# A quarter of the FFN's inner layer on 32-column places of the TensorE array

## The chip, the cores and the metric

The kernel runs on one core of one Trainium2 chip. The metric is device time in microseconds, from one launch; the time before is the median of three runs.

## The reference

The input x has 10000 rows of 512 values. A graph layer comes first (message passing over 5000 edges, two linear layers with batch norm and SiLU), then a mixture-of-experts layer. The change touches only the second, which with tokens normalised per row and grouped by 16 is:

```python
cont_logits = einsum('bgtd,des->bgtes', grouped, controller) + tie
cont_perm = (cont_logits == max(cont_logits, axis=-3, keepdims=True))
intermediate = einsum('bgtd,desf->bgtesf', grouped, f1)
inner = relu(einsum('bgtesf,bgtes->bgesf', intermediate, cont_perm))
inter2 = einsum('bgesf,esfd->bgesd', inner, f2)
result = einsum('bgesd,bgtes->bgtd', inter2, cont_perm)
```

There are 16 x 4 = 64 expert sets (called experts here). In each group of 16 tokens each expert picks the token with the largest logit, multiplies it by its own 512 x 32 matrix (the inner layer), and by its own 32 x 512 matrix (the outer layer); the result goes back to the token that was picked.

## The kernel before

The graph layer fills about the first 1278 us. The FFN follows: its 10000 tokens are cut into 20 chunks of 512 (`CH`; the last has 272), each with `G` = 32 groups of 16 tokens. Matrices `f1_sb` and `f2_sb` stay in SBUF.

A loop of `step` calls works as a pipeline written out by hand: one call (a round) handles five chunks at different stages. Chunk `a` is normalised, transposed (`flip`) and gets its logits and choice; chunk `b` gathers the picked tokens and runs the inner layer; chunk `d` runs the outer layer; chunk `e` is turned and scattered back; later chunks load. Inside the FFN each engine's instructions keep their program order (`InOrder`; all such instructions have the line 525 of that helper in the profile, so they are told apart by their tiles).

The part around the change goes over `k`, the four 128-row slices of the 512 inputs:

```python
gat(1); inn(0); turns(2, 4)
gat(2); inn(1); turns(4, 6)
gat(3); turns(6, 8); silu(0); silu(1)
inn(2); silu(2); silu(3)
inn(3); put(b, Chunk.relu); put(e, Chunk.scatter, 0)
```

(written here in fewer lines). `gather(k)` multiplies token tiles `xl` by the one-hot table `bd` on TensorE into PSUM (`pb`), and ScalarE copies the result to `gs`: for slice k, 128 inputs by 64 experts by 32 groups. `inner(k, gs)` multiplies this by `f1_sb` and adds up over k in the PSUM tile `pi`, two banks of 128 partitions by 16 blocks `m` by 2 by 32 groups. A block m holds four experts, and is computed in two matmuls, one for q = 0 (partitions 0 to 63) and one for q = 1 (partitions 64 to 127). Each has the weights of two experts (s = 0 and 1, 2 x 32 = 64 array columns) and as moving operand the tokens of both (2 x 32 = 64 columns). So each matmul yields four 32 x 32 squares, and two of them, the weights of one expert with tokens of the other, are not used: `relu` reads only rows 64q + 32s with column half s. The two matmuls lie on different columns of the array, and are free to run side by side.

`outer` then reads the result `ib` with matmuls of 32 rows by 32 columns; `scatter` uses 64 rows by 32 columns, `gather` 32 rows by 128 columns, `logits` 128 by 64, `flip` and `residual` are transposes of 128 by 128. The profile writes these shapes as 32*32, 64*32, 32*128, 128*64 and 128*128, and behind them the rows by the moving columns.

Of the kernel before, what the change touches and what calls it, by code (L numbers as in the profile page):

```python
# [18 lines left out]
NEX, SETS, F = 16, 4, 32  # L19
# [4 lines left out]
KH = H // P  # L24
# [26 lines left out]
def gnn_ffn_kernel(ctx: ExitStack, tc: tile.TileContext, a: dict, out: bass.AP):  # L51
# [126 lines left out]
    with tc.tile_pool(name="pe1", bufs=1) as pe1, tc.tile_pool(name="pe", bufs=2) as pe, \  # L178
# [31 lines left out]
        for r0 in range(0, AGG_ROWS, 8 * P):  # L210
            j = min(8, (AGG_ROWS - r0) // P)
# [39 lines left out]
        for g in range(groups):  # L251
            row = targets(g)
            for i in range(EG):
                t = g * EG + i
# [27 lines left out]
        for g in range(groups):  # L282
# [3 lines left out]
            for i in range(EG):  # L286
                t = g * EG + i
                nc.vector.tensor_scalar(same[i], row[:, :i + 1, :], dst_f[:, t:t + 1], None, op0=ALU.is_equal)
            rs, sh = ln
            for i in range(EG):  # L290
                t = g * EG + i
# [8 lines left out]
            for i in range(EG):  # L300
                t = g * EG + i
                pc = ps_e.tile([TE, H], F32, name="pc", bufs=3)
                for k in range(i, EG):
                    nc.tensor.matmul(pc, lhsT=same[k][:, i, :], rhs=xgs[g * EG + k], start=(k == i),
                                     stop=(k == EG - 1))
# [204 lines left out]
    f1_sb = wf.tile([P, KH, ES * F], F32, name="f1_sb")  # L510
# [16 lines left out]
    pe, dve, act, pool = (InOrder(e) for e in (nc.tensor, nc.vector, nc.scalar, nc.gpsimd))  # L527

    class Chunk:
# [148 lines left out]
        def inner(self, k, gs):  # L678


            if k == 0:
                self.pi = ps_i.tile([P, MF, 2, G], F32, name="pi")
            gs = gs.rearrange("p (t u q s b) g -> p t u q b s g", t=2, u=4, q=2, s=2)
            for m in range(MF):
                for q in range(2):
                    b, t = m // 2, m % 2
                    j = 4 * b + 2 * q + t
                    pe.matmul(self.pi[64 * q:64 * q + 64, m], lhsT=f1_sb[:, k, 2 * F * j:2 * F * (j + 1)],
                                     rhs=gs[:, t, b // 2, q, b % 2],
                                     start=(k == 0 and m % 8 == 0), stop=(k == KH - 1), skip_group_check=True)  # L690

        def relu(self):

# [268 lines left out]
```

## Time and profile before

| | us |
|---|---|
| median of three runs | 1968.99 (1967.05 to 1970.73) |
| the profiled execution | 1968.09 |
| its span, first to last instruction | 1966.4 |
| start of the first inner-layer matmul | 1278.8 |
| TensorE busy, share of the span | 1792.2, 91% |
| VectorE busy | 1207.8, 61% |
| ScalarE busy | 722.5, 37% |
| GpSimd busy | 621.5, 32% |
| inner-layer matmuls busy | 165.9, 5120 records of 225 ns mean |
| mean granted TensorE clock | 0.967 |

A record is one entry of the trace. TensorE's records overlap: the mean of one is from its start to its end, and neighbours on other columns or rows run beside it, so 5120 records of 225 ns come to 165.9 us of busy time. What a record costs in a stream is the distance between starts, not its length. In the page's lines PE is TensorE's matmuls, PEld its weight loads, DVE VectorE, ACT ScalarE, POOL GpSimd, SP the queue that issues DMAs; `<-` after an idle time names what ended it.

### The profile page before, as it was taken

What the parts mean: (1) busy time and instruction counts of PE and PEld (TensorE: products, weight loads), DVE (VectorE), ACT (ScalarE), POOL (GpSimd) and SP (SyncE); (2) the same over time, 40 slices, a digit from 0 to 9 for tenths busy, and PEclk for the clock granted to TensorE, in tenths of its full rate; (3) what the DMA queues carried; (4) which work ended last, traced back from release to release, by engine and by line L of the source; (5) the groups of instructions that cost most, each with busy time, mean ns of one, the idle gap of its engine ahead of it and who ended that gap; (6) DMA issues with size and microseconds to landing.
All of it is one profiled execution on the core that took longest, in us unless ns stands there. A gap on an engine that the chain in (4) does not pass through costs nothing. (4 is left out here: it accounts for less than half of the span.)

```text
span 1966.4 us, 43924 instructions
## 1 busy us (share of the span) xinstructions
PE 1792.2 (91%) x19354; PEld 1029.4 (52%) x19354; DVE 1207.8 (61%) x1894; ACT 722.5 (37%) x973; POOL 621.5 (32%) x626
## 2 busy tenths in 40 slices
PE   5959399999999997999999999589999999999985
PEld 2424144444444443444444444367777777777763
DVE  8547276777777767434334334327787777777766
ACT  0324233333333315222222220255555555555432
POOL 4275333333233314333333331122323232323311
PEclk9979599999999998999999999699999999999998
DMA  9997444443444312333333331742232323232101
GB/s 349 301 228 143 99 169 170 162 158 151 162 162 162 140 42 84 125 147 128 143 125 126 125 126 42 237 129 88 87 112 79 120 79 120 80 119 70 45 24 57
DMA packets 95219, 256.37 MB, mean 130 GB/s; under 512 B 7845, under 2 KB 8435, under 8 KB 94452
## 3 DMA queue, kind: packets, MB, share of 16 engines
q1 hardware_dynamic: 86068, 232.58, 32.5%
q0 software_dynamic: 8960, 20.98, 5.3%
q8 instruction: 152, 2.49, 0.5%
q14 instruction: 39, 0.32, 0.0%
HBM read 143.47 MB, written 110.07 MB: 129 GB/s over the span
## 5 line engine op out<-in xcount | busy, mean ns | idle before, releaser
L133 PE MATMUL x<-h_s,w_u 128*128 128x500 f32 x640 | 289.1, 584 | 0.3 <-POOL h_s L123 0.3
L525 ACT COPY gs<-pb 128x1024 f32<-128x1024 f32 (+2 forms) x168 | 161.5, 1027 | 123.6 <-PE pb L525 112.0
L133 PEld LDWEIGHTS x<-h_s,w_u 128*128 128x128 f32 x640 | 122.4, 191 | 148.2 <-issue 142.9
L525 DVE STREAM_TRANSPOSE it<-it 128x1024 f32<-128x1024 f32 x152 | 174.9, 1209 | 0.1
L525 PE MATMUL pi<-gs,f_sb 128*64 128x64 f32 x5120 | 165.9, 225 | 3.3 <-ACT gs L525 1.7
L525 POOL TENSOR_TENSOR pv<-perm,odd_t 64x512 f32<-64x512 f32 (+1 forms) x80 | 99.8, 1248 | 206.8 <-PE pb L525 178.2
L525 PEld LDWEIGHTS pi<-gs,f_sb 128*64 128x64 f32 x5120 | 157.3, 140 | 11.0 <-issue 2.2
L525 PE MATMUL pb<-bd,xl 32*128 32x128 f32 x2504 | 144.7, 285 | 15.1 <-ACT it L525 8.8
L143 DVE SCALAR_TENSOR_TENSOR t<-w,s 128x500 f32<-128x500 f32 x60 | 40.7, 678 | 188.5 <-PE w L133 184.8
L133 PE MATMUL z<-h_s,w 128*128 128x500 f32 x320 | 148.3, 586 | 3.9 <-POOL h_s L123 3.9
L525 PE MATMUL pb<-f_sb,ib 32*32 32x256 f32 x5120 | 134.7, 385 | 14.2 <-ACT it L525 8.6
L525 DVE COPY it<-pb 128x1024 f32<-128x1024 f32 x76 | 93.1, 1225 | 88.6 <-PE pb L525 88.5
L133 PE MATMUL z<-h_s,w_u 128*128 128x500 f32 x320 | 144.0, 583 | 0.3 <-POOL h_s L123 0.3
L525 PEld LDWEIGHTS pb<-bd,xl 32*128 32x128 f32 x2504 | 129.0, 188 | 27.7 <-ACT it L525 13.6
L123 POOL TENSOR_TENSOR h_s<-hc 128x500 f32<-128x500 f32 x60 | 77.0, 1316 | 149.1 <-PE z L133 149.1
L525 ACT COPY it<-pb 128x1024 f32<-128x1024 f32 x76 | 79.0, 1039 | 112.1 <-PE pb L525 112.1
L138 ACT COPY s<-z 128x500 f32<-128x500 f32 x60 | 34.5, 575 | 220.2 <-PE z L133 156.4
L525 POOL TENSOR_SCALAR ln_rs<-ln_mv 128x4 f32<-128x4 f32 (+2 forms) x22 | 4.9, 224 | 302.5 <-DVE ln_mv L525 302.4
L525 PEld LDWEIGHTS pb<-f_sb,ib 32*32 32x32 f32 x5120 | 70.2, 103 | 57.1 <-ACT it L525 14.6
L133 PEld LDWEIGHTS z<-h_s,w_u 128*128 128x128 f32 x320 | 60.8, 190 | 73.9 <-issue 72.7
L123 POOL TENSOR_TENSOR h_s<-hb 128x1000 f32<-128x1000 f32 x30 | 69.6, 2335 | 91.5 <-PE z L133 65.3
L433 DVE BATCH_NORM_STATS2 st<-h 128x6 f32<-128x500 f32 x144 | 93.7, 671 | 1.3
(180 smaller groups left out, 3084.9 us busy)
## 6 DMA issues: line engine op xcount, KB each, us to landing
h1s<-h SPq DMA_DIRECT2D x36, 1000.0 KB
agg<-zero SPq DMA_DIRECT2D x10, 2048.0 KB
xt<-in_x_dram SPq DMA_DIRECT2D x20, 1000.0 KB
hc<-h1s SPq DMA_DIRECT2D x20, 1000.0 KB
h2s<-h SPq DMA_DIRECT2D x20, 1000.0 KB
x<-in_x_dram SPq DMA_DIRECT2D x39, 512.0 KB
out_dram<-x SPq DMA_DIRECT2D x39, 512.0 KB
yt<-h2s SPq DMA_DIRECT2D x76, 256.0 KB
```

The lines of the kernel that those rows point to most:

```text
L123: eng.tensor_tensor(t[:, k0:k1], q(*x0, k0, k1), q(*x1, k0, k1), op)
L133: nc.tensor.matmul(bank, lhsT=us[n][:, k, m * P:(m + 1) * P], rhs=bs[n][k], start=start and k == 0, stop=k == kb - 1, skip_group_check=True)
L138: nc.scalar.copy(kept[n], banks[n])
L143: nc.vector.scalar_tensor_tensor(dst, banks[x0], sc, kept[x1], op0=op, op1=ALU.add)
L433: nc.vector.bn_stats(out=st1[:, 4 * r + m, 2 * i + t, :], in_=h1[:, r, t, :])
L525: return lambda *args, **kw: tc.keep_in_program_order(f(*args, **kw))
```

## The change

In `inner`, of each four blocks the second (m = 1, 5, 9, 13) is computed with one expert to a matmul: four matmuls, each with 32 array columns (one expert's weights) and 32 moving columns (the same expert's tokens), on the four 32-column places of the array. The squares that nobody reads are no longer computed in these blocks. The other twelve blocks stay at two matmuls of 64 columns. The order over m and q, the PSUM tile and its readers stay.

```diff
             for m in range(MF):
+                b, t = m // 2, m % 2
+                alone = m % 4 == 1
                 for q in range(2):
-                    b, t = m // 2, m % 2
-                    j = 4 * b + 2 * q + t
-                    pe.matmul(self.pi[64 * q:64 * q + 64, m], lhsT=f1_sb[:, k, 2 * F * j:2 * F * (j + 1)],
-                                     rhs=gs[:, t, b // 2, q, b % 2],
-                                     start=(k == 0 and m % 8 == 0), stop=(k == KH - 1), skip_group_check=True)
+                    es = 8 * b + 4 * q + 2 * t
+                    for s in (0, 1) if alone else (slice(0, 2),):
+                        e0, e1 = (es + s, es + s + 1) if alone else (es, es + 2)
+                        c0 = 64 * q + F * (e0 - es)
+                        pe.matmul(self.pi[c0:c0 + F * (e1 - e0), m, s], lhsT=f1_sb[:, k, F * e0:F * e1],
+                                  rhs=gs[:, t, b // 2, q, b % 2, s],
+                                  start=(k == 0 and m % 8 == 0), stop=(k == KH - 1), skip_group_check=True)
```

## The prediction

> **What bounds the kernel now.** I read the page's busy table first, then the busy time of two rounds of the FFN loop, then TensorE's waits in that loop, then the order of time on TensorE.
>
> The busy table and the group that the change edits (busy us, mean ns of one; then the engine's idle time before them):
>
> ```profile
> PE 1792.2 (91%) x19354; PEld 1029.4 (52%) x19354; DVE 1207.8 (61%) x1894; ACT 722.5 (37%) x973; POOL 621.5 (32%) x626
> ...
> L525 PE MATMUL pi<-gs,f_sb 128*64 128x64 f32 x5120 | 165.9, 225 | 3.3 <-ACT gs L525 1.7
> ```
>
> TensorE is busy 91% of the span. The inner layer has 5120 records for 20 chunks x 4 slices of D x 32 matmuls = 2560 matmuls, so each fp32 matmul is two records ("passes" below). They began only 3.3 us late in total. 128*64 says 128 rows and 64 columns of the array; 128x64 says 64 moving columns.
>
> Busy time by stretch, two rounds of the loop (a round handles one chunk per stage and takes about 32.8 us):
>
> ```profile
> core 0: us, PE busy (x) PEld busy (x) DVE busy (x) ACT busy (x) POOL busy (x), PEclk, DMA share, GB/s
> ...
> 1600.00:1633.00 33.00, 31.87 (x819) 24.38 (x818) 24.96 (x34) 18.53 (x23) 9.82 (x12) 1.00 0.32 99
> ...
> 1700.00:1733.00 33.00, 32.21 (x826) 24.77 (x824) 25.23 (x34) 18.64 (x23) 9.81 (x12) 1.00 0.31 100
> ```
>
> TensorE is busy 32.2 of 33.0 us at a granted clock of 1.00; VectorE, the next, 25.2. What TensorE waited for in the loop, 1300 to 1900 us (total us, times, longest):
>
> ```profile
> PE pb L525 <- ACT it L525: 13.1, 32, 1.1
> ...
> PE pb L525 <- ACT gs L525: 0.6, 1, 0.6
> ```
>
> The only wait of size is in the outer layer, for a PSUM buffer that ScalarE empties; around the inner layer there is next to none. So TensorE bounds the loop, and time added to the inner layer adds to the round.
>
> Now TensorE in order of time (start us, length us):
>
> ```profile
> 1602.36 2.09 PE L525 MATMUL pi<-gs,f_sb 128*64 128x64 f32 x64
> 1604.37 1.72 PE L525 MATMUL pb<-bd,xl 32*128 32x128 f32 x32
> ...
> 1609.69 3.95 PE L525 MATMUL pi<-gs,f_sb 128*64 128x64 f32 x128
> 1613.57 0.67 PE L525 MATMUL pb<-it,pv 64*32 64x256 f32 x16
> ```
>
> A run of 64 inner records takes 1604.37 - 1602.36 = 2.01 us until the next kind starts, one of 128 takes 3.88. The difference, 1.87 us for 64, makes 29.2 ns a record; two places of 64 columns work side by side, so a pair takes 58.4. What is left, 2.01 - 1.87 = 0.14 us, is paid once a run, whatever its length. It is the price of changing the shape of the array. Two other kinds give it as well:
>
> ```profile
> 1617.20 1.09 PE L525 MATMUL ps<-ident,xl 128*128 128x128 f32 x8
> 1618.22 1.90 PE L525 MATMUL pb<-f_sb,ib 32*32 32x256 f32 x64
> ...
> 1620.06 0.65 PE L525 MATMUL pi<-xlt,ctl 128*64 128x256 f32 x4
> 1620.64 0.66 PE L525 MATMUL ps<-ident,xl 128*128 128x128 f32 x4
> ...
> 1621.23 0.65 PE L525 MATMUL pi<-xlt,ctl 128*64 128x256 f32 x4
> ...
> 1623.82 1.08 PE L525 MATMUL pi<-xlt,ctl 128*64 128x256 f32 x8
> 1624.83 0.66 PE L525 MATMUL ps<-ident,yt 128*128 128x128 f32 x4
> ```
>
> Transposes (128*128): eight take 1.02 us, four 0.59, so 0.43 for four more and 0.16 a run. Logits (128*64, 256 moving columns): eight take 1.01, four 0.58, so 0.43 for four more and 0.15 a run. Both have 128 rows: a change of column size alone, from 64 to 128 or back, pays 0.15 us too, though no row size changed.
>
> **The change part by part.** In each of the 80 calls of `inner` (20 chunks x 4 slices), blocks m = 1, 5, 9 and 13 turn from two matmuls of 64 array columns and 64 moving columns into four of 32 and 32: 80 x 4 = 320 changed blocks. 640 matmuls go, 1280 come; TensorE gets 640 more matmuls, which is 1280 more records, each with a weight load. The order of instructions on VectorE, ScalarE, GpSimd and the DMA queue is the same before and after; no wait is added, and buffers, `relu` and all readers of `pi` stay. [...]So the whole sum is TensorE's.
>
> *Removed:* 4 records a block, 4 x 29.2 = 117 ns.
>
> *Added records:* 8 a block on four places. No row shows 128*32 with 32 moving columns (four transposes of the last chunk have 128*32, with 128 columns on one place). By the slope of the rows: a pair of 256-column records takes 0.43/2 = 215 ns, a pair of 64-column ones 58.4, so 0.816 ns a moving column, and 58.4 - 32 x 0.816 = 32.3 ns at 32. If four places work at once, two passes take 65 ns; this is the low end, since faster would mean streaming faster than any row. If only two places ever overlap, four sets take 129: the high end. Between them lies the nearest kind with 32-column places and short operands, the last scatter:
>
> ```profile
> 1955.18 1.18 PE L525 MATMUL pb<-f_sb,pv 64*32 64x64 f32 x64 [0.99 <-DVE f_sb L525]
> ```
>
> (1.18 - 0.31) / 63 = 13.8 ns a record (0.31 us is the mean of one in its group), 110 ns for eight, but with twice the moving columns and eight places. I take 80 ns: the low end, plus some 13 ns because four starts follow each other at about 6.5 ns, as the two of a pair do now.
>
> A rule bears on this. The Trainium skill, "TensorE: Matmul & The Clock Gate", section "Wait — 56ns, not 53.3ns?", says that start to start never drops below about 25 ns however small the matmul. The row above has 13.8 ns on separate places, so the floor does not hold from place to place; I go by the row. By the rule the eight records would take 200 ns, and my sum would rise by 0.12 x 308 = 37 us.
>
> *Added changes of shape:* every changed block lies between blocks of 64 columns (m = 0 and 15 are not changed). The run is broken twice, into 32 columns and back: 640 more changes. For the way back I take 0.14, the price of the inner layer's own runs. For the way in, no row has this pair of shapes; the three prices are 0.14 to 0.16, and they contain the first weight load, which is shorter for fewer columns (means of 103, 140 and 190 ns for 32, 64 and 128 columns). I take 0.13, with 0.12 and 0.16 as ends. Below that, to nothing, is the third rival.
>
> A second rule speaks for the change: the Trainium skill, "TensorEngine Tiling (Array Packing)", section "Theoretical Speedup", gives up to 4x for a dimension of 32 or less against up to 2x at 64. Blocks would fall to half, 117 to 59 ns, 320 x 58 = 19 us saved. The run prices above are what it leaves out: 270 ns a block stand against those 58.
>
> *Sum per block:* 0.13 + 0.14 + 0.080 - 0.117 = +0.233 us, or 3.7 us a round of 16 blocks.
>
> *What hides some.* In the last round the chunk has 272 tokens and TensorE waits for ScalarE's copies:
>
> ```profile
> 1914.07 2.09 PE L525 MATMUL pi<-gs,f_sb 128*64 128x64 f32 x64 [1.66 <-ACT gs L525]
> ```
>
> The 12 changed blocks of the first three slices there run inside such waits, the last four do not. 320 - 12 = 308 blocks x 0.233 = 72 us. In the other rounds I count nothing hidden: the next gather, and then the scatter, follow the inner layer with no wait. VectorE and ScalarE get later work and more slack. At most the idle 0.8 us of each round, 18 x 0.8 = 14 us, could be taken up, if waits for `it` shrank; I use it for the low end only. Next late is VectorE's `relu`, which waits for `pi`, and with it everything in the following round by the same 3.7 us.
>
> The sum is against the profiled execution: 1968.09 us (span 1966.4 and 1.7 around it), 0.9 below the median of 1968.99, which is inside the spread of the runs. The same difference on the median: 1969 + 72 = 2041 us.
>
> **The rivals.**
>
> 1. *Forecast:* each changed block pays two changes of shape. 2041 us. Chance 0.80.
> 2. *Records in line:* 25 ns each by the rule, or places that hold each other up: 0.13 + 0.14 + 0.20 - 0.117 = 0.353, x 308 = 109, so 2078 us. For it: rule, and 110 ns for eight in the scatter where streaming alone would allow less. Against it: 13.8 ns a record. Chance 0.05.
> 3. *One change of shape free:* 32-column places lie inside the 64-column ones, so only one of the two directions might pay: 0.14 + 0.080 - 0.117 = 0.103, x 308 = 32, so 2001 us. Against: transposes and logits pay both ways. Chance 0.06.
> 4. *No price between 64 and 32 columns* (the other side; also if both widths run in the same shape, so that the change is less than it says): 0.080 - 0.117, or 0.065 - 0.117, x 320 = -12 to -17, so 1952 to 1957 us. It decides at the price of a change of shape: with 80 ns of records a block breaks even at (117 - 80) / 2 = 18 ns a change. The cheapest of three kinds is 140. Chance 0.09.
>
> **How the numbers follow.** Low end of the forecast: 0.12 + 0.14 + 0.065 - 0.117 = 0.208 x 308 = 64, less the 14 us of idle time: +50, 2019 us. High end: 0.16 + 0.16 + 0.129 - 0.117 = 0.332 x 308 = 102, 2071 us; I stop at 2070. Rivals 2 to 4, together 0.20, lie outside. A difference below 0.2% (4 us) can't be told from none. Slower by more than that: cases 1 to 3 less a sliver, 0.90; within it 0.01; faster 0.09.
>
> **What would show it.** Right: the inner layer's records fall into two groups, 128*64 x3840 and 128*32 x2560; a round grows from 32.8 to about 36.5 us; from the last record of 64 columns to the first of 32 there are about 150 ns (58 within a run), and some 0.12 back; the other engines' busy times stay. Wrong: records of 32 columns starting 50 ns or less after those of 64 (rival 4), or in only one direction late (rival 3), or 25 ns apart from each other (rival 2); or a round that grows by much less than 16 x 0.233 us while TensorE's waits for `it` shrink, which would say that I took too little as hidden.

## The result, and the profile after

| | before | changed |
|---|---|---|
| median of six runs, us | 1966.2 (1964.8 to 1970.7) | 2060.3 (2051.5 to 2067.9) |
| profiled execution, us | 1968.09 | 2054.67 |
| its span, us | 1966.4 | 2053.0 |
| mean granted TensorE clock in it | 0.967 | 0.953 |

The changed kernel is slower: ratio 1.0474, 95% interval 1.044 to 1.0508, or 94 us between the medians and 86.6 between the two profiled spans. The forecast was +72, so the time lies inside the stated range and above its middle. The runs of the changed kernel also spread wider, 16 us against 6.

The busy table of the changed kernel's page, and its two inner-layer groups with shapes kept apart:

```profile
PE 1883.9 (92%) x20634; PEld 1076.6 (52%) x20634; DVE 1205.6 (59%) x1894; ACT 720.8 (35%) x973; POOL 623.0 (30%) x626
```

```profile
L525 PE MATMUL pi<-gs,f_sb 128*64 128x64 f32 x3840 | 203.8, 239 | 1.4 <-issue 1.4
...
L525 PE MATMUL pi<-gs,f_sb 128*32 128x32 f32 x2560 | 87.6, 210 | 0.0
```

TensorE has 20634 - 19354 = 1280 more records, split as announced, 3840 and 2560. VectorE, ScalarE and GpSimd are busy as long as before to within 2.2 us. All of the time is in TensorE's stream.

A round in the middle of the loop, by busy time (columns as before), and TensorE's waits between 1310 and 1890 us:

```profile
1606.60:1643.10 36.50, 35.71 (x888) 26.54 (x886) 25.02 (x34) 18.56 (x23) 9.85 (x12) 1.00 0.26 90
```

```profile
PE pb L525 <- ACT it L525: 11.6, 30, 0.6
PE ps L525 <- DVE x L525: 1.2, 2, 1.0
PE pi L525 <- ACT xlt L525: 0.9, 1, 0.9
```

The same waits of the kernel before:

```profile
PE pb L525 <- ACT it L525: 12.1, 31, 0.5
PE ps L525 <- issue: 1.4, 2, 0.8
PE pi L525 <- ACT xlt L525: 0.9, 1, 0.9
PE pb L525 <- ACT gs L525: 0.6, 1, 0.6
```

A round takes 36.5 us in place of 32.8. The waits for `it` total 11.6 us; before, they were 12.1. So no wait gave room for the added time. In order of time, the same round:

```profile
1606.88 3.00 PE L525 MATMUL pi<-gs,f_sb 128*64 128x64 f32 x80
1609.82 1.72 PE L525 MATMUL pb<-bd,xl 32*128 32x128 f32 x32
...
1616.05 5.79 PE L525 MATMUL pi<-gs,f_sb 128*64 128x64 f32 x160
1621.77 1.53 PE L525 MATMUL pb<-it,pv 64*32 64x256 f32 x48
```

(Both shapes are merged in these lines, under the name of the first.) A call until the next gather takes 1609.82 - 1606.88 = 2.94 us; it was 2.01. The difference, 0.93 us, over four blocks is 0.23 us a block. The weight loads of its first blocks, of which the first of each line starts 2 ns before its matmul (the last line stops after six):

```profile
1606.88 0.20 PEld L525 LDWEIGHTS pi<-gs,f_sb 128*64 128x64 f32 x4
...
1607.14 0.16 PEld L525 LDWEIGHTS pi<-gs,f_sb 128*32 128x32 f32 x8
...
1607.34 0.26 PEld L525 LDWEIGHTS pi<-gs,f_sb 128*64 128x64 f32 x6
```

Single starts in the trace show where the time goes, the same to 1 ns at every change in the loop at full clock. The first 32-column record starts 152 ns after the last 64-column one (52 from pair to pair inside a run). The four places start 7 ns apart, and their second pass 52 ns after the first. The first 64-column record starts 126 ns after the last 32-column one, and the next pair 100 ns after that pair (again 52 inside a run). Streaming takes some 53 ns for 64 columns and 27 for 32, estimated from the 215 ns that 256 columns take in the logits; so 99 ns are left at each change, in either direction, in which nothing starts. The late second passes, 48 ns for 64 columns and some 20 for 32, fit a first weight load that nothing covers; that was not tried by itself.

The rounds at the two ends behave otherwise. These are stretches of the kernel before, the first round and then everything from the start of the last inner layer:

```profile
1278.80:1309.70 30.90, 23.20 (x438) 19.18 (x436) 8.90 (x20) 14.24 (x19) 4.71 (x8) 1.00 0.58 176
1901.70:1966.40 64.70, 40.67 (x1326) 27.98 (x1324) 43.20 (x37) 17.18 (x26) 8.23 (x8) 0.90 0.12 44
```

and the same two of the changed kernel:

```profile
1279.80:1317.90 38.10, 34.03 (x500) 25.97 (x498) 8.84 (x20) 14.19 (x19) 4.73 (x8) 0.73 0.43 134
1972.20:2053.00 80.80, 59.97 (x1390) 37.34 (x1388) 43.30 (x38) 17.18 (x26) 8.24 (x8) 0.58 0.10 35
```

The column before the last two is the granted clock. It fell from 1.00 to 0.73 in the first round and from 0.90 to 0.58 at the end. The first round grew by 7.2 us and the end by 16.1, where four blocks in each of four calls would explain 3.7 in each. In all, the 86.6 us divide into 1.0 before the FFN, 7.2 in the first round, 60.7 in the next seventeen, 1.6 in the one after (around its start the kernel before itself ran at half clock for 6.8 us), and 16.1 at the end.

### The profile page after: what moved, and what is told of

It reads as the page before. It is cut to its first block, busy times and chain, and to the rows that moved or that the text cites. A ratio compares the mean times of both kernels' runs of the same rounds, so it can differ in the third digit from the quotient of the medians.

```text
span 2053.0 us, 46484 instructions
## 1 busy us (share of the span) xinstructions
PE 1883.9 (92%) x20634; PEld 1076.6 (52%) x20634; DVE 1205.6 (59%) x1894; ACT 720.8 (35%) x973; POOL 623.0 (30%) x626
## 4 chain that ended last, share of the span: by engine, by line
PE 70%; DVE 8%; DMA 7%; ACT 5%; POOL 4%; SPq 3%; issue 2%; POOLq 0%; ACTq 0%; DVEq 0%
PE pb L525 17%; PE pi L525 14%; PE x L133 9%; PE z L133 9%; PE w L133 5%; PE v L133 5%; PE ps L525 3%; PE y L133 3%; SPq L212 3%; DVE ln_st L354 2%; ACT xt L365 2%; ACT it L525 2%; DMA L_ffn_controller_sb<-in_L_ffn_controller_dram 2%; PE pt L133 2%; DVE st L433 2%
## 5 line engine op out<-in xcount | busy, mean ns | idle before, releaser
L525 PE MATMUL pi<-gs,f_sb 128*64 128x64 f32 (+1 forms) x6400 | 246.4, 227 | 1.4 <-issue 1.4
L525 PEld LDWEIGHTS pi<-gs,f_sb 128*64 128x64 f32 (+1 forms) x6400 | 201.2, 130 | 45.6 <-issue 2.2
L525 PE MATMUL pb<-f_sb,ib 32*32 32x256 f32 x5120 | 141.6, 406 | 13.7 <-ACT it L525 9.2
L525 PEld LDWEIGHTS pb<-bd,xl 32*128 32x128 f32 x2504 | 129.3, 189 | 24.9 <-ACT it L525 14.0
L525 DVE TENSOR_SCALAR ib<-pi 32x512 f32<-32x512 f32 x40 | 27.2, 681 | 138.6 <-PE pi L525 138.3
L133 PEld LDWEIGHTS z<-h_s,w_u 128*128 128x128 f32 x320 | 60.7, 190 | 74.0 <-issue 72.9
```

Source lines behind the costliest of these rows:

```text
L133: nc.tensor.matmul(bank, lhsT=us[n][:, k, m * P:(m + 1) * P], rhs=bs[n][k], start=start and k == 0, stop=k == kb - 1, skip_group_check=True)
L525: return lambda *args, **kw: tc.keep_in_program_order(f(*args, **kw))
```

## The experiments

Ratios are to the kernel before in the same set of runs, with 95% intervals. Theory A: the price is the change of array shape, paid in each block. Theory B: the small records themselves cost. For what goes beyond 20 x 3.7 us, theory C: the broken stream holds the clock at half in the end rounds.

**All blocks on 32-column places.**

```diff
-                alone = m % 4 == 1
+                alone = True
```

> All 16 blocks on 32-column places with one expert each, so no change of array shape inside a call. Theory (the price is the change of shape, 99 ns of emptying plus the uncovered first weight load, twice a block; the 32-column records themselves cost 32 ns a set of four): a call takes about 16 x 65 ns = 1.04 us in place of 1.87, 0.83 less, 80 calls, at most 66 us less than before, about 1900; with some of it lost to waits for ScalarE's copies of the gather and for VectorE's transposes, 1900 to 1930. Rival (the small records themselves are what costs, 230 ns a block): four times the loss of the quarter, +94 x 4, about 2340.

Measured: 2071.6 us, 1.0527 (1.0492 to 1.0562). Both expectations missed. Part of A held: an undisturbed call takes 1.23 us (1770.99 to 1772.22 below), 0.78 less than before. But TensorE then stands still. Its waits from 1300 to 2000 us, and a piece in order of time:

```profile
PE pi L525 <- issue: 73.1, 50, 2.6
PE pb L525 <- issue: 15.1, 16, 2.2
```

```profile
1770.99 1.30 PE L525 MATMUL pi<-gs,f_sb 128*32 128x32 f32 x128
1772.22 1.15 PE L525 MATMUL pb<-bd,xl 32*128 32x128 f32 x15
1775.15 1.29 PE L525 MATMUL pb<-bd,xl 32*128 32x128 f32 x17 [1.78 <-issue]
1776.37 1.72 PE L525 MATMUL pi<-gs,f_sb 128*32 128x32 f32 x111
1778.62 0.44 PE L525 MATMUL pi<-gs,f_sb 128*32 128x32 f32 x17 [0.54 <-issue]
...
1782.03 3.00 PE L525 MATMUL pi<-gs,f_sb 128*32 128x32 f32 x207
1786.11 0.87 PE L525 MATMUL pi<-gs,f_sb 128*32 128x32 f32 x49 [1.09 <-issue]
```

88 us of waits that no semaphore explains. Between the first two, 17 + 111 = 128 records (each with its weight load 256 instructions); between the next two about 256. All through the loop the distance between stalls is a multiple of 128, give or take the few records that a trace loses. The DMA part of the page counts the transfers that bring instructions (packets, MB, share), before and then here:

```profile
q8 instruction: 152, 2.49, 0.5%
```

```profile
q8 instruction: 192, 3.15, 0.6%
```

Each packet is 3.15 MB / 192 = 16.4 KB. All instruction transfers of this page, 3.15 + 0.32 MB, over its 54164 instructions make 64 bytes each, so a packet holds 256. In the loop these packets start no closer than 3.2 us in any kernel here, and the closest tenth of this one lies between 3.2 and 3.5 us. The stalls fall at the ends of these blocks: a block can be used up in 1.2 us, and the next is not there. The packets' own times agree: between 1300 and 1900 us TensorE starts nothing for over 0.9 us 49 times, and 47 of these gaps end 1.2 to 1.6 us after a packet has landed. Stalls also drop the clock (mean 0.934), which stretches the rest.

**The same four blocks, put last in a call.**

```diff
-            for m in range(MF):
+            for m in [m for m in range(MF) if m % 4 != 1] + [m for m in range(MF) if m % 4 == 1]:
```

> The same four blocks on 32-column places as in the changed kernel, but put at the end of each call, after the twelve others: one more change of shape in a call (and one back, only between the last two calls of a round) in place of eight. Theory (change of shape): 12 x 117 + 0.12 + 4 x 65 ns = 1.78 us a call against 1.87 before, so 4 to 7 us less than before, about 1961. Rival (small records cost by themselves): as the changed kernel, about 2060. In between if streaming of successive sets is slower than 32 ns.

Measured: 1968.0, 1.0007 (0.9989 to 1.0024). The records are the changed kernel's to the last one, only their order differs, and the loss is gone. That is the test between A and B, and B falls. But the 4 to 7 us that A expected to gain did not come; they lie outside the interval. One call and the next gather:

```profile
1602.34 2.01 PE L525 MATMUL pi<-gs,f_sb 128*64 128x64 f32 x80
1604.28 1.72 PE L525 MATMUL pb<-bd,xl 32*128 32x128 f32 x32
```

A call takes 1.94 us against 2.01, so the gain is there in a call. From 1310 to 1890 us the inner layer's calls add up to 139.0 us against 142.0 before (distance between starts), and the scatter to 65.4 against 61.7: what the calls gain, the scatter behind them loses. Why the scatter is slower was not tried here; the version with eight such blocks, below, shows the same more strongly.

**As many records, no change of shape.**

```diff
-                        e0, e1 = (es + s, es + s + 1) if alone else (es, es + 2)
+                        e0, e1 = es, es + 2
```

> In the same blocks four matmuls of 32 moving columns, as in the changed kernel, but each with the weights of both experts on a 64-column place: as many records as in the changed kernel, half the moving columns of before each, and no change of shape. Theory (change of shape): two places, so four sets of two in a block at 32 ns if streaming bounds them (+13 ns a block, +4 us, 1970), up to 57 if the 64-column weight load bounds them (+112 ns, +36 us, 2002). Rival (number of records, issue): as the changed kernel, about 2050 to 2060.

Measured: 2005.5, 1.0186 (1.0154 to 1.0217), +39 us, just above A's upper end. A call:

```profile
1621.23 2.60 PE L525 MATMUL pi<-gs,f_sb 128*64 128x64 f32 x80
1623.76 1.72 PE L525 MATMUL pb<-bd,xl 32*128 32x128 f32 x32
```

2.53 - 2.01 = 0.52 us over four blocks, 0.13 a block: four sets of two take 0.25 us, about 60 ns a set, as much as with 64 moving columns. On a 64-column place the time of a set does not shrink with the moving columns. That the weight load sets it is likely, and was not tried by itself.

**The change in the middle chunks alone, and at the ends alone.**

```diff
-                alone = m % 4 == 1
+                alone = m % 4 == 1 and 0 < self.c < NC - 2
```

> The change in chunks 1 to 17 alone; chunks 0, 18 and 19 keep 64 columns in all blocks. The loss in a full round of the middle is 3.68 us in the traces (36.47 against 32.79). Theory (what the loss has beyond 20 x 3.68 comes from more time at half clock in the first and the last rounds): 17 x 3.68 = 63 us, about 2029, granted clock as before (0.967), spread as narrow as before. Rival (the excess is in the middle rounds too or comes from elsewhere): 17/20 of the whole loss, 80 us, about 2046.

Measured: 2030.9, 1.0313 (1.028 to 1.0345), +65 us for 17 chunks, 3.8 each, and runs within 4 us of each other. The other half has `not 0 < self.c < NC - 2`:

> The change in chunks 0, 18 and 19 alone; chunks 1 to 17 keep 64 columns in all blocks. Theory (broken streams of 32- and 64-column blocks hold the clock at half once it has fallen, in the first and last rounds where TensorE also pauses): 3 x 3.7 = 11 us for the blocks and some 18 to 30 us for the clock, about 1995, clock about 0.95, with the wide spread of the changed kernel. Rival (only the blocks' price): 11 us, about 1977, clock 0.967.

Measured: 1990.6, 1.0117 (1.0085 to 1.0149), +27 us for three chunks, 9 each, runs from 1981 to 1996 at clocks of 0.954 to 0.961. 65 and 27 make 92 of the 94 us. The blocks at the ends cost more than twice what they cost in the middle.

**At the ends alone, but put last in a call** (both edits together).

> As the version with the change in chunks 0, 18 and 19 alone, with the same matmuls, but with the four 32-column blocks put behind the others in each call, so that the stream is broken once in place of eight times. Theory (it is the broken stream that holds the clock at half after a pause): clock 0.967 or more, time within 5 us of before, about 1965, spread narrow. Rival (32-column blocks or the larger number of records hold the clock down, or the rounds at the ends vary by themselves): 10 us or more slower, clock about 0.955.

Measured: 1969.7 over 20 runs, 1.0011 (0.9999 to 1.0023). The same matmuls in the same chunks, +3 us in place of +27. So neither 32-column blocks nor the number of records hold the clock down; the broken order does. C stands, with a limit: the expected narrow spread did not come (1964 to 1979), and single runs of the kernel before also reach 1976 at a clock of 0.957. The profiled run here took 1977.3 us, and its clock is at half for 30.7 us in the outer layer, where no stream is broken. So the end of the kernel can fall to half clock by itself. With the broken order all four runs were slower (1981 to 1996) than any of these 20.

**Half as many broken places.**

```diff
-                alone = m % 4 == 1
+                alone = m % 8 == 5
```

> Two blocks in 16 (m = 5 and 13) on 32-column places in all chunks, in their own place: half as many changes of shape. Theory: 0.230 us a block, 1.84 us a round, 17 middle rounds 31 us; the three rounds at the ends 5.5 us, and at most the 18 us that the clock cost there with four blocks, so 2002 to 2022. If the clock falls for long only when the stream is broken often, 2003; if any break will do, 2020.

Measured: 2007.4, 1.0217 (1.0194 to 1.0239), +41 us. A full round takes 34.63 us in the trace, 1.84 more than before, exactly half of 3.68. The blocks alone would give 37. The time lies between the two cases: the fastest run (2000.6) has a clock of 0.968 and no long fall in its trace, the two slowest (2010 and 2013) have 0.959.

**Fewer blocks in 32 columns without a broken stream: can the gain of a call be had?** Three versions, all slower. Eight blocks, put last (`m % 2 == 1`):

> Every second block on 32-column places, the eight put after the other eight in each call. By streaming alone: 8 x 117 + 0.12 + 8 x 65 ns = 1.58 us a call against 1.87, one more change of shape between the last two calls of a round: about 20 us less than before, 1946. Theory of instruction supply (TensorE's instructions come in 16 KB blocks of 128 matmul records with their weight loads, and all blocks on 32 columns outran them, a block every 3.5 us at best): 96 records a call are borderline, some stalls, between 1950 and 1990. Rival (the loss of the version with all blocks is from waits for ScalarE's copies): no stalls marked issue, 1946.

Measured: 1996.7, 1.0164 (1.0141 to 1.0186). All blocks in slices k = 0 and 2 (`alone = k % 2 == 0`):

> All 16 blocks on 32-column places, but only in slices k = 0 and 2; slices 1 and 3 keep 64 columns. No extra change of shape except between the last two calls. By streaming alone: 40 calls x 0.83 us = 33 us less, 1933 to 1940. Supply theory: as many instructions as with every second block, in shorter bursts, some stalls of 1 to 2.7 us: 1940 to 1990. Rival (ScalarE's copies): 1935 to 1945, no stalls marked issue.

Measured: 2002.1, 1.0192 (1.0162 to 1.0221). All blocks in slice 0 (`alone = k == 0`):

> All 16 blocks on 32-column places in slice k = 0 alone. By streaming alone: 20 calls x 0.83 us = 16 us less, 1950. Supply theory: 64 more records a round with the same gather around them, mostly in the reserve that the instruction queue has: 1950 to 1965, few stalls. It would be the one version here that beats both kernels.

Measured: 1981.0, 1.0091 (1.0057 to 1.0125), outside both expectations; it was to be the best. Where no stall comes, the gain is had: its shortest rounds in the middle take 32.01 us against 32.79. But others take up to 39.1, and TensorE waits 12.7 us for instructions from 1310 to 1890 us. The waits in the same stretch with eight blocks:

```profile
PE pb L525 <- ACT it L525: 13.2, 34, 0.5
PE pb L525 <- issue: 10.0, 16, 1.2
PE pi L525 <- issue: 8.7, 13, 1.5
```

18.7 us of waits for instructions, where the kernel before has 1.4 in that stretch. The waits for ScalarE's copies, the rival cause, are 13.2 us for `it` and 0.6 for `gs`; they were 12.1 and 0.6. (With all blocks in slices 0 and 2 the waits for `gs` are 4.2 us, beside 22.7 for instructions; there the rival has a small part.) And the shortage does not stay in the inner layer: the scatter, 128 records in a row, takes 4.8 us a round with eight blocks and 3.6 before (distance between starts).

**All blocks on 32 columns, two slices left out.**

```diff
+            if k > 1:
+                return
```

(with `alone = True`, and the sum ending at k = 1)

> All blocks on 32-column places, but the inner layer's products of slices k = 2 and 3 are left out (the gathers stay), so the output is not the layer's. The records of a round are as many as before the change (820), in short bursts of 128. Supply theory (the number of instructions outran the 16 KB blocks when all blocks were on 32 columns): hardly any wait of TensorE marked issue in the loop (under 10 us in total, 88 with all four slices), a round of 26 to 28 us. Rival (the 32-column bursts themselves stall the instruction stream): half of the waits remain, 35 to 50 us, a round of 29 to 31 us.

Measured: one run, 1978.6 us, clock 0.933; waits marked issue 22.3 + 10.6 = 33 us from 1300 to 1900 us, rounds of 31 to 35 us after the first. Neither expectation holds; the waits come close to the rival's. With four slices they were 74.9 us in the same stretch, so half of the bursts left 44% of the waits. It is not the number of records in a round that decides, as I had put it, but how fast a burst uses them: a gather and a burst together still ask for 160 records in less than 3.4 us. TensorE also waited 18 us for VectorE's transposes, a bound that the longer inner layer had covered. How far ahead instructions are fetched, and why the blocks start 3.4 us apart, stays open; the transfer of one takes only about 1.0 us in the traces.

## Why the prediction was right, and where its sum was short

**The price of a block** came out: +0.233 us forecast, 3.68 / 16 = 0.230 measured. In its parts: the two changes of shape and their first weight loads were put at 270 ns, read off runs of other kinds. The starts show 99 ns at each change in which nothing starts, plus late second passes of about 48 ns for 64 columns (100 instead of 52) and 20 for 32 (52 instead of 32), 266 in all. The slope's 32.3 ns for a set of 32 moving columns is 32 to 35 in the runs of such records. A block's eight records take 72 ns from first start to last; with 27 for the last one's streaming, and without the 20 already counted, that is 79, where I had 80.

**Nothing hidden in the middle rounds** was right: the starts give 16 x 0.230 us a round, and a full round grew by 3.68. TensorE's listed waits from 1310 to 1890 us shrank only from 15.0 to 13.7 us in total.

**The rivals.** Records in line at 25 ns: starts lie 7 ns apart. One free direction: both pay 99 ns. No price between 64 and 32 columns: the same 99. The grouped version, with only the order changed, rules out the first and the third of these too: its records are the same, and the loss is gone. That both directions pay is read from the starts alone.

**The step that was short** is the one on what hides, together with the silent assumption that a broken stream leaves the clock as it was in all 20 rounds. I took 2.8 us off for the last round, because TensorE waits there for ScalarE. In fact the three rounds at the ends cost 24.9 us in the profiled pair (7.2 + 1.6 + 16.1), and 27 in the version with the change at the ends alone, instead of the 3 x 3.7 - 2.8 = 8 in the sum. The seventeen rounds between cost 60.7, where the sum had 63. What the trace shows there is the clock. Its record knows two rates, 1.0 and 0.5, and the falls that the end of the run does not cut short last 3.4 us or multiples (6.8, 20.5, 23.9, 30.7). In the end rounds TensorE pauses, for instructions in the first and for ScalarE in the last, and the clock falls. In the first round it stayed at half for 20.5 us with the broken stream, and did not fall at all before, though TensorE paused there too. At the start of the last round it was back after 3.4 us before; with the broken stream it stayed at half for 23.9 us. The row is:

```profile
1971.90:1996.00 24.10, 24.10 (x405) 19.35 (x408) 13.72 (x12) 4.46 (x13) 0.00 (x0) 0.51 0.01 2
```

TensorE busy 24.10 of 24.10 us, at a clock of 0.51. The Trainium skill, "TensorE: Matmul & The Clock Gate", section "What's actually happening", has the full clock return after one busy window of some 3.4 us. By that the half clock there would cost, as an estimate from the page's figure, half a window, 1.7 us. This trace differs: until the outer layer's second run of matmuls (1921.18 us before, 2000.12 after) the last round grew by 8.5 us, of which the blocks explain 3.7. A likely reason is that busy by the profile's count is not busy for the clock: at half clock 244 ns pass before the first 32-column record and 172 before the first 64-column one, 137 and 119 more than streaming at half speed takes, so some 256 of each 1107 ns are empty (two changes in four blocks). That emptiness is what counts is argued; that the order of the blocks decides is shown by the two versions at the ends. The other 7.6 of the 16.1 us come after that point, where no block was changed: the outer layer runs at half clock for another 30.7 us, as it also does in the profiled run of the version with the blocks put last at the ends. Everything after the last inner layer, before and then changed:

```profile
1916.00:1966.40 50.40, 28.98 (x1038) 16.94 (x1034) 31.23 (x28) 13.15 (x14) 8.23 (x8) 0.90 0.15 55
```

```profile
1996.00:2053.00 57.00, 36.17 (x1000) 18.17 (x984) 29.88 (x26) 12.73 (x14) 8.24 (x8) 0.62 0.14 49
```

(The first begins with the scatter, the second 2 us into it.) How far the broken stream brings on this second fall is not shown.

My sum could have seen the danger in the clock of 0.90 in the last stretch of the kernel before: the clock already fell there at times, for 3.4 and for 10.2 us.

The price of a block and the middle rounds were right for the reason given. That the time fell inside 2019 to 2070 in spite of the clock is luck: the range was wide at the top because it took in a high price for records, and that was not the cause of the excess.

## What to carry to other kernels

A small matmul that saves half its streaming is worth nothing if its neighbours have another array shape: count the changes of shape before the saved columns, and keep equal shapes together. Before a matmul stream is cut finer, hold its instructions per microsecond against what the instruction queue brings; here bursts that used 128 matmul records in much less than 3.4 us ran dry. In rounds where TensorE pauses, allow for half clock over the whole stream once it is broken: in the last round here that was 23.9 us in place of 3.4.

## What the runs showed of the hardware that I had not expected

- Instructions come in 16 KB packets, and in the loop no two started less than 3.2 us apart in any kernel here. 128 records with their weight loads per 3.4 us are 27 ns a record; the inner layer before the change, at 29 ns a record, was already close to that.
- A change of array shape costs the same 99 ns from 64 to 32 columns and from 32 to 64 at full clock, beyond the streaming of the last record (137 and 119 at half clock).
- Four 32-column places of 128 rows, with 32 moving columns, take 32 to 35 ns a set and start 7 ns apart; two 64-column places with the same 32 moving columns take about 60.
- The clock can stay at half for 24 us while the profile shows TensorE busy without a break.
